# Column tiles of 64 or 32 for the plain products, and transposes in 64-row halves, in a four-layer transformer on one core

## The chip, the cores and the metric

The kernel runs on one core of a Trainium2 chip. A core has TensorE (PE; its weight loads are shown as PEld), VectorE (DVE), ScalarE (ACT), GpSimd (POOL) and SyncE (SP), which run side by side and wait for one another through semaphores. The metric is the device time of one execution in microseconds; the median of several runs is compared.

## The reference, cut to what matters

The input is `x`, 16 sequences of 256 tokens of 128 features, in float32. Four layers follow; each is an attention and a feed-forward part, both on the layer-normed `x` and both added to `x`.

```python
x = x + L0_attn(ln(x))   # 16 heads of 64, l2-normed q and k, ALiBi, causal, 2 null keys per head
x = x + L0_ffn(ln(x))    # gelu(x @ w1 + b1) @ w2 + b2, 512 wide
x = x + L1_attn(ln(x))   # 16 heads of 8 from a latent of 64, one shared k and v, causal
x = x + L1_ffn(ln(x))    # silu(w1 x) * (w2 x), two gelu layers of 512x512, w3
x = x + L2_attn(ln(x))   # 16 heads of 64, no mask, biases
x = x + L2_ffn(ln(x))    # each token through the best of 8 experts (relu, 512 wide)
x = x + L3_attn(ln(x))   # 16 heads of 8, causal, window of 128
x = x + L3_ffn(ln(x))    # token shift, sigmoid(r) * (relu(k)^2 @ W_v)
```

Layers 0 and 2 are called wide here (heads of 64), layers 1 and 3 narrow (heads of 8). All products are in float32.

## The kernel before, in words

Everything stays on the chip: the 4096 tokens lie in eight tiles `xg[g]` of two sequences each (a sequence is called a batch, `b`). Each batch of a layer goes through a preparation (`prep0` to `prep3`: layer norm, transpose of the normed tile by `turned`, projections to queries, keys and values), through units of heads (`wide_unit`, four per batch; `narrow_unit`, three per batch) and through an output step (`wide_out`, `narrow_out`; `out0` adds the null part of layer 0). After every second batch comes the feed-forward part of its tile (`feed0`, `feed1`, the gate and the experts in `Experts`, `mix`).

A unit has three kinds of work on TensorE: scores (queries against keys, contraction over 64 rows, or over 32 in the narrow layers), transposes of the probabilities, and products of transposed probabilities and values. Between them stand the softmax steps on DVE, ACT and POOL.

None of this is issued where it is written. Each piece is a `step` of the class `Plan`: an engine, a rank `p`, an estimated duration, the values that it reads and writes, and a function that emits its instructions. `Plan.run` (L132) builds one order for all engines from these: it follows the estimated times, gives out the buffers ("homes"), and takes the step that can start soonest, the lower rank first. PSUM is the home "t", eight banks of 512 columns. A step with the engine "AD" (the copies out of PSUM, `evac`, L392) may go to ACT or DVE, whichever the estimates favour.

A step of PE carries a mode, which names the tile of the 128x128 array that its matmuls use:

- "T": the whole array, 128 rows by 128 columns. All plain products (projections, feed-forward, experts, output) and the transposes of whole blocks are of this mode.
- "S": tiles of 64 rows. Wide scores and the half transposes of `turned_halves` (L367), which turn the upper and the lower 64 rows of a block into two different banks.
- "S4": tiles of 32 rows. Narrow scores.
- "O": tiles of 64 columns. Wide products of probabilities and values.
- "O4": tiles of 32 columns. Narrow products of probabilities and values.

Some matmuls have another shape than their step's mode says: the null part of layer 0, `nv_out` with 32 rows and its transposes to 32 partitions, lies inside "T" steps.

The planner counts `SWITCH` (130 ns) for a change of mode on PE, lets PE stay in its mode for a step up to `STAY` ranks later, and takes no step that is over `WINDOW` (12) ranks ahead of the first unfinished step of PE that is not of mode "T". `TURN` limits how far a step may take a buffer ahead of a lower-ranked step that is short of it.

All plain products go through one helper, and whole blocks are turned by one loop:

```python
def mm(o, lhsT, rhs, start=True, stop=True, **kw):
    nc.tensor.matmul(o, lhsT, rhs, start=start, stop=stop, **kw)
...
def turn(e):
    for i in range(nt):
        nc.tensor.transpose(t.t[:, i * P:(i + 1) * P], xn.t[:, i * D:(i + 1) * D], ident)
```

In the profile, L365 is the helper `mm`, L372 is `turned_halves`, L429 is the transpose in `turned`, L618 and L641 are those of `narrow_out`, L388 and L390 are the copies on ACT and DVE, L479 divides probabilities on POOL, L566 is the first softmax step of a narrow unit.

Of the kernel before, what the change touches and what calls it, by code (L numbers as in the profile page):

```python
# [67 lines left out]
class Plan:  # L68
# [11 lines left out]
    WINDOW, STAY, TURN, SWITCH = 12.0, 4.0, 3.0, 130  # L80
# [51 lines left out]
    def run(self):  # L132
        free = dict.fromkeys(self.SEEN, 0.0)
        ready = {e: [] for e in free}
        by_rank = sorted((s for s in self.steps if s.eng[0] == "PE" and s.mode != "T"), key=lambda s: (s.p, s.no))
        at, mode, left, window = 0, None, len(self.steps), self.WINDOW

# [25 lines left out]
        while left:  # L163
# [11 lines left out]
            for e, steps in ready.items():  # L175
# [12 lines left out]
                if e == "PE":  # L188
                    low = min(c[1] for c in could if c[0] <= soon + 40)
                    could = [(max(t, free[e] + self.SWITCH) if s.mode != mode else t, p, n, s) for t, p, n, s in could  # L190
                             if s.mode != mode or p <= low + self.STAY]
                    soon = min(could)[0]
# [18 lines left out]
            if e == "PE":  # L211
                mode = s.mode
# [19 lines left out]
def preln_d4_kernel(ctx: ExitStack, tc: tile.TileContext, x_in, vecs, rows, nullk, nullv,  # L232
# [127 lines left out]
    plan.home("small", many(sp, "small", 5, [256]))  # L360
    plan.home("pn", many(sp, "pn", 3, [2, 16, 2]))


    def mm(o, lhsT, rhs, start=True, stop=True, **kw):
        nc.tensor.matmul(o, lhsT, rhs, start=start, stop=stop, **kw)  # L365
# [57 lines left out]
    def turned(p, xn, nt, gamma=None):  # L423

        t, xnT = get("t"), get("xnT")

        def turn(e):
            for i in range(nt):
                nc.tensor.transpose(t.t[:, i * P:(i + 1) * P], xn.t[:, i * D:(i + 1) * D], ident)  # L429

        step("PE", p, 109 * nt, turn, r=[xn], w=[t], mode="T")
        n = nt * P
        if gamma is None:
            evac(p, xnT, t, lambda: (xnT.t[:, 0:n], t.t[:, 0:n]), n)
        else:
            step("ACT", p - 8, n * 0.83 + 145, lambda e: nc.scalar.activation(xnT.t[:, 0:n], t.t[:, 0:n], AF.Copy, scale=gamma),
                 r=[t], w=[xnT])
        return xnT
# [80 lines left out]
    def wide_out(p, b, st, w_out, more=None, reads=()):  # L519
        y = get("t")  # L520
        for qc in range(2):
# [8 lines left out]
            step("PE", p + 0.5 * qc, 1800 + (420 if more else 0), part, r=st["OT"] + list(reads), w=[y], mode="T")  # L530
# [81 lines left out]
    def narrow_out(p, b, st, w_proj):  # L612
# [3 lines left out]
        def turn(e):  # L616
            for i in range(4):
                nc.tensor.transpose(t.t[:, i * P:(i + 1) * P], oT.t[:, i * P:(i + 1) * P], ident)  # L618
# [18 lines left out]
        t2, yT = get("t"), get("small")  # L637

        def turn2(e):
            for qc in range(2):  # L640
                nc.tensor.transpose(t2.t[:, qc * P:(qc + 1) * P], o_sb.t[:, qc * P:(qc + 1) * P], ident)  # L641

        step("PE", p + 1, 218, turn2, r=[o_sb], w=[t2], mode="T")
        evac(p + 1, yT, t2, lambda: (yT.t[:, 0:256], t2.t[:, 0:256]), 256)
# [6 lines left out]
        step("PE", p + 2, 450, project, r=[yT], w=[y], mode="T")  # L651
# [44 lines left out]
    nv_out = cp.tile([32, D], F32, tag="nv_out", name="nv_out")  # L696
# [7 lines left out]
    def null2(e):  # L704
# [6 lines left out]
    step("PE", -13, 20, lambda e: nc.tensor.transpose(nk_ps.t[:, 0:16], nsq.rearrange("p j d -> p (j d)"), ident[0:16, 0:16]),  # L711
         r=["nss"], w=[nk_ps], mode="T")
# [9 lines left out]
    step("PE", 2, 2000, null3, w=[nv_ps], mode="T")  # L722
    step("DVE", 2, 200, lambda e: nc.vector.tensor_copy(nv_out, nv_ps.t[0:32, 0:D]), r=[nv_ps], w=["nv_out"])
# [3 lines left out]
    def prep0(b):  # L727
# [15 lines left out]
        def project(n, c):  # L743
# [6 lines left out]
                 r=[xnT], w=[ps], mode="T")  # L750
# [35 lines left out]
        def values(k):  # L786
# [3 lines left out]
                 r=[xnT], w=[ps], mode="T")  # L790
# [28 lines left out]
    def out0(b, st):  # L819
        p = first[0, b] + 12 + 13  # L820
        t, pnT = get("t"), get("small")

        def turn(e):
            for qc in range(2):
                nc.tensor.transpose(t.t[0:32, qc * P:(qc + 1) * P], st["pn"].t[:, qc].rearrange("p h n -> p (h n)"), ident)

        step("PE", p - 1, 218, turn, r=[st["pn"]], w=[t], mode="T")
        evac(p - 1, pnT, t, lambda: (pnT.t[0:32, 0:256], t.t[0:32, 0:256]), 256)
        wide_out(p, b, st, wout, lambda y, qc: mm(y[:, qc * P:(qc + 1) * P], pnT.t[0:32, qc * P:(qc + 1) * P], nv_out, False, True),
                 reads=[pnT, plan.key("nv_out")])  # L830
# [5 lines left out]
    def feed0(g):  # L836
# [9 lines left out]
        for c in range(4):  # L846
            ps = get("t")
            step("PE", lo + 6 + 2 * c, 862, lambda e, c=c, ps=ps: mm(ps.t, wA[:, o1 + c * P:o1 + (c + 1) * P], xnT.t),
                 r=[xnT, "wA"], w=[ps], mode="T")
# [8 lines left out]
        for i in range(4):  # L858
# [4 lines left out]
            step("PE", lo + 18 + i, 896, down, r=h + ["wA"], w=[y], mode="T")  # L863
# [3 lines left out]
    for b in range(B):  # L867
        st = prep0(b)

        def nulls_kept(p, u, pair, pr, st=st):  # L870

            def f(e):
                for qc, (a, z) in enumerate(parts0):
                    nc.gpsimd.tensor_copy(st["pn"].t[:, qc, 4 * u + 2 * pair:4 * u + 2 * pair + 2, :], pr.t[:, :, a:a + 2])
# [27 lines left out]
    def prep1(b):  # L902
# [6 lines left out]
        step("PE", lo + 5, 431, lambda e: mm(ps.t[:, 0:256], wl[:, at1["down"]:at1["down"] + P], xnT.t[:, 0:256]), r=[xnT], w=[ps], mode="T")  # L909
# [7 lines left out]
        step("PE", lo + 6, 862, both, r=[lat], w=[ps2], mode="T")  # L917
# [8 lines left out]
        step("PE", lo + 7, 450, values, r=[lat], w=[ps3], mode="T")  # L926
# [18 lines left out]
    def feed1(g):  # L945
# [8 lines left out]
        for c in range(4):  # L954
# [11 lines left out]
            step("PE", p, 1724, up, r=[xnT, "w1", f"h2.{g - 1}"], w=[pa, pb], mode="T")  # L966
# [4 lines left out]
        def layer(name, sname, src, p):  # L971
            dst = [get("r") for _ in range(4)]
            for o in range(4):
                ps = get("t")
                for half in range(2):
# [4 lines left out]
                    step("PE", p + 2 * o + half, 1724, hidden, r=src, m=[ps], w=[f"{name}.{g}"], mode="T")  # L980
# [531 lines left out]
```

## Time and profile before

| what | us |
|---|---|
| median of 3 runs (2195.37 to 2201.18) | 2196.09 |
| the profiled execution | 2192.15 |
| its span, first to last instruction | 2190.5 |
| PE busy, 26001 matmul records | 2097.8 |
| ACT busy | 1695.0 |
| DVE busy | 1633.5 |
| POOL busy | 1049.6 |

The times of single stages come from one profiled execution. A matmul in float32 leaves two records, one for each of two passes, and a transpose one. Records of matmuls overlap, since they are pipelined: the distance from one start to the next tells how long the array was taken, and the duration does not. By the scores, layer 0 runs from about 47 to 630 us of the span, layer 1 to 1133, layer 2 to 1816 (its second half of experts to about 1985, beside the beginning of layer 3), and layer 3 to the end.

### The profile page before, as it was taken

The page shows a single profiled execution, that of the slowest core. Times are in us where ns is not written, and L with a number is a line of the kernel's source. Part 1 is how long each engine was busy: PE and PEld are TensorE (multiplying, and loading weights), DVE is VectorE, ACT ScalarE, POOL GpSimd, SP SyncE. Part 2 cuts the span into 40 slices and gives each one's busy share as a digit, 9 for nine tenths or more (in the row PEclk, how much of TensorE's full clock was granted, in tenths as well). Part 3 has the DMA queues.
Part 4 walks back from the last instruction along what each step waited for, and adds up shares of the span by engine and source line. Part 5 has one row for each costly group of instructions (what it writes and reads, how often), then busy time and mean ns, then how long its engine had stood idle before and what let it go on. Part 6 is the DMA issues. An engine that isn't in the chain of part 4 may idle for free. (4 is left out here: it accounts for less than half of the span.)

```text
span 2190.5 us, 68042 instructions
## 1 busy us (share of the span) xinstructions
PE 2097.8 (96%) x26001; PEld 1519.2 (69%) x26001; DVE 1633.5 (75%) x6363; ACT 1695.0 (77%) x4798; POOL 1049.6 (48%) x2019
## 2 busy tenths in 40 slices
PE   5999999999999999999999999999999999998996
PEld 3667777776776555555566677888888786786664
DVE  5898898889888666556655456767665788887996
ACT  4898889889889877678667667777766677777995
POOL 5997798788851111111113335554443855226331
PEclk9999999999999999999999999999999999999998
DMA  8000000000000000000000000000332000451000
GB/s 188 32 2 2 2 2 2 2 2 2 30 13 3 2 2 2 2 2 2 2 1 2 1 2 7 7 6 5 119 112 84 26 5 19 138 163 30 12 13 12
DMA packets 58488, 57.92 MB, mean 26 GB/s; under 512 B 27809, under 2 KB 48817, under 8 KB 58161
## 3 DMA queue, kind: packets, MB, share of 16 engines
q1 hardware_dynamic: 55360, 48.54, 7.9%
q8 instruction: 205, 3.36, 0.7%
q0 software_dynamic: 2048, 4.20, 0.6%
q14 instruction: 123, 1.00, 0.2%
q10 hardware_dynamic: 752, 0.83, 0.1%
HBM read 43.32 MB, written 10.22 MB: 24 GB/s over the span
## 5 line engine op out<-in xcount | busy, mean ns | idle before, releaser
L447 POOL TENSOR_TENSOR x<-x,row_sb 128x256 f32<-128x256 f32 x48 | 35.0, 730 | 43.8 <-DVE xn0x L416 18.5
L409 POOL TENSOR_SCALAR ln_rs2x<-ln_mv2x 128x2 f32<-128x2 f32 x21 | 4.0, 191 | 72.6 <-DVE ln_mv2x L405 71.9
L409 POOL TENSOR_SCALAR ln_rs3x<-ln_mv3x 128x2 f32<-128x2 f32 x23 | 4.4, 191 | 68.1 <-DVE ln_mv3x L405 63.9
L409 POOL TENSOR_SCALAR ln_rs1x<-ln_mv1x 128x2 f32<-128x2 f32 x23 | 5.2, 226 | 64.9 <-DVE ln_mv1x L405 63.9
L409 POOL TENSOR_SCALAR ln_rs4x<-ln_mv4x 128x2 f32<-128x2 f32 x23 | 4.4, 191 | 65.3 <-DVE ln_mv4x L405 60.9
L409 POOL TENSOR_SCALAR ln_rs0x<-ln_mv0x 128x2 f32<-128x2 f32 x22 | 4.2, 191 | 64.8 <-DVE ln_mv0x L405 63.4
L1001 POOL TENSOR_TENSOR x<-x,sq1x 128x512 f32<-128x512 f32 x4 | 5.1, 1266 | 62.4 <-DVE sq1x L999 62.4
L479 POOL TENSOR_SCALAR probs4x<-probs4x,sums2x 128x256 f32<-128x256 f32 (+2 forms) x44 | 23.0, 536 | 25.0 <-DVE sums2x L474 18.1
L376 POOL TENSOR_TENSOR ss0x<-ss0x,mhalf 128x16 f32<-128x16 f32 x11 | 32.0, 2909 | 5.7 <-DVE ss0x L756 4.3
L376 POOL TENSOR_TENSOR ss1x<-ss1x,mhalf 128x16 f32<-128x16 f32 x11 | 32.3, 2938 | 2.8 <-DVE ss1x L756 2.7
L376 POOL TENSOR_TENSOR ss2x<-ss2x,mhalf 128x16 f32<-128x16 f32 x11 | 31.9, 2902 | 3.6 <-DVE ss2x L756 3.1
L376 POOL TENSOR_TENSOR ss3x<-ss3x,mhalf 128x16 f32<-128x16 f32 x11 | 32.2, 2930 | 0.1
L479 POOL TENSOR_SCALAR probs4x<-probs4x,sums4x 128x256 f32<-128x256 f32 (+2 forms) x44 | 20.3, 475 | 24.7 <-DVE sums4x L474 24.3
L479 POOL TENSOR_SCALAR probs0x<-probs0x,sums6x 128x256 f32<-128x256 f32 (+2 forms) x44 | 19.2, 453 | 25.8 <-DVE sums6x L474 18.7
L479 POOL TENSOR_SCALAR probs4x<-probs4x,sums6x 128x256 f32<-128x256 f32 (+2 forms) x40 | 17.6, 454 | 27.2 <-DVE sums6x L474 19.9
L479 POOL TENSOR_SCALAR probs2x<-probs2x,sums6x 128x256 f32<-128x256 f32 (+2 forms) x44 | 19.4, 455 | 23.2 <-DVE sums6x L474 16.0
L376 POOL TENSOR_TENSOR ss5x<-ss5x,mhalf 128x16 f32<-128x16 f32 x10 | 29.8, 2979 | 1.3 <-DVE ss5x L756 1.2
L479 POOL TENSOR_SCALAR probs0x<-probs0x,sums2x 128x256 f32<-128x256 f32 (+2 forms) x40 | 18.6, 478 | 24.4 <-DVE sums2x L474 24.3
L376 POOL TENSOR_TENSOR ss4x<-ss4x,mhalf 128x16 f32<-128x16 f32 x10 | 29.0, 2900 | 2.4 <-DVE ss4x L756 2.0
L479 POOL TENSOR_SCALAR probs2x<-probs2x,sums4x 128x256 f32<-128x256 f32 (+2 forms) x40 | 19.2, 491 | 22.5 <-DVE sums4x L474 22.1
L479 POOL TENSOR_SCALAR probs2x<-probs2x,sums2x 128x256 f32<-128x256 f32 (+2 forms) x44 | 21.0, 490 | 15.7 <-DVE sums2x L474 15.5
L479 POOL TENSOR_SCALAR probs2x<-probs2x,sums0x 128x256 f32<-128x256 f32 (+2 forms) x44 | 19.6, 460 | 17.1 <-DVE sums0x L474 14.8
(4452 smaller groups left out, 10747.5 us busy)
## 6 DMA issues: line engine op xcount, KB each, us to landing
w0x<-in_wex_dram SPq DMA_DIRECT2D x16, 578.0 KB, 3.9
w1x<-in_wex_dram SPq DMA_DIRECT2D x15, 578.0 KB, 4.1
w2x<-in_wex_dram SPq DMA_DIRECT2D x15, 578.0 KB, 4.0
w_wA<-in_wa_dram SPq DMA_DIRECT2D x8, 512.0 KB, 5.7
ex_rows<-zero SPq DMA_DIRECT2D x2, 1472.0 KB, 22.4
x<-in_x_dram SPq DMA_DIRECT2D x8, 256.0 KB, 7.8
w_wB<-in_wb_dram SPq DMA_DIRECT2D x4, 512.0 KB, 6.6
xs0x<-ex_rows SPq DMA_DIRECT2D x16, 64.0 KB, 3.7
```

What stands on the lines that cost most here:

```text
L376: nc.gpsimd.tensor_tensor(t, t, mhalf[:t.shape[0]].broadcast_to([t.shape[0], n]), ALU.pow)
L409: nc.gpsimd.tensor_scalar(ln.t[2], ln.t[1][:, :, 1], LN_EPS, 1.0, ALU.add, ALU.mult)
L447: step("POOL", p, 670, lambda e: nc.gpsimd.tensor_tensor(x_of(b), x_of(b), row_over(name, 2), ALU.add), r=reads, m=[X[b]])
L479: nc.gpsimd.tensor_scalar(pr.t[:, j, a:z], pr.t[:, j, a:z], sums.t[:, i:i + 1], 1.0, ALU.mult, ALU.mult)
L1001: step("POOL", lo + 30, 1300, lambda e: nc.gpsimd.tensor_tensor(x, x, ys.t.rearrange("p (c d) -> p c d", d=D), ALU.add), r=[ys, "w1"], m=xx)
```

## The change

The mode "T" of the plain products becomes a mode "P", which has no tile of its own. When such a step is taken, it uses the column tiles that PE is already in (64 columns in "O", 32 in "O4"); if PE is in another mode, it uses that of the next unfinished products of probabilities and values. `mm` then issues each product as two or four matmuls, one for each column tile, on the same moving data. `flip` turns a block in column tiles by a product with the identity; the transposed tokens of the experts use it.

```diff
+    COLUMNS = {"O": 64, "O4": 32}
+    WINDOW, STAY, TURN, SWITCH = 20.0, 4.0, 4.0, 180
-    WINDOW, STAY, TURN, SWITCH = 12.0, 4.0, 3.0, 130
...
-        by_rank = sorted((s for s in self.steps if s.eng[0] == "PE" and s.mode != "T"), key=lambda s: (s.p, s.no))
+        by_rank = sorted((s for s in self.steps if s.eng[0] == "PE" and s.mode != "P"), key=lambda s: (s.p, s.no))
...
+        def tiling(s):
+
+            if s.mode != "P":
+                return s.mode
+            return mode if mode in self.COLUMNS else next((x.mode for x in by_rank[at:] if x.end is None and x.mode in self.COLUMNS), "O")
...
+    def parts(n):
+
+        w = plan.COLUMNS.get(plan.mode, P)
+        return [slice(a, min(n, a + w)) for a in range(0, n, w)]
 
     def mm(o, lhsT, rhs, start=True, stop=True, **kw):
-        nc.tensor.matmul(o, lhsT, rhs, start=start, stop=stop, **kw)
+        for c in parts(o.shape[0]):
+            nc.tensor.matmul(o[c], lhsT[:, c], rhs, start=start, stop=stop, **kw)
+
+    def flip(o, block):
+
+
+        i = ident[0:block.shape[0], 0:block.shape[0]]
+        if plan.mode in plan.COLUMNS:
+            mm(o, block, i)
+        else:
+            nc.tensor.transpose(o, block, i)
```

The transposes of whole blocks become half transposes of mode "S", each into two banks with two copies out: those of `turned` (all layer norms), of `mix`, of `out0` and the second ones of `narrow_out`. The first ones of `narrow_out` (L618) keep the mode "T" and the whole array.

```diff
+    def in_halves(p, src, n, out_of):
+
+        t = [get("t"), get("t")]
+
+        def turn(e):
+            for i in range(n):
+                turned_halves(t, 64 * i, src[1](i))
+
+        step("PE", p, 62 * n, turn, r=[src[0]], w=t, mode="S")
+        return [(t[z], lambda z=z: t[z].t[:, 0:64 * n].rearrange("p (i q) -> p i q", q=64),
+                 lambda z=z: out_of().rearrange("p (i z q) -> p i z q", z=2, q=64)[:, :, z]) for z in range(2)]
...
     def turned(p, xn, nt, gamma=None):
...
+        xnT = get("xnT")
+        for t, src, dst in in_halves(p, (xn, lambda i: xn.t[:, i * D:(i + 1) * D]), nt, lambda: xnT.t[:, 0:nt * P]):
+            if gamma is None:
+                evac(p, xnT, t, lambda src=src, dst=dst: (dst(), src()), nt * 64)
```

The null part is padded from 32 to 128 rows with zeros: `pn` has 128 columns for each half of the queries, `nv_out` 128 rows. To make room, "pn" has two buffers for three and "small" four for five.

```diff
-    plan.home("small", many(sp, "small", 5, [256]))
-    plan.home("pn", many(sp, "pn", 3, [2, 16, 2]))
+    plan.home("small", many(sp, "small", 4, [256]))
+    pn = many(sp, "pn", 2, [2, P])
+    for t in pn:
+        nc.gpsimd.memset(t, 0.0)
+    plan.home("pn", pn)
...
-    nv_out = cp.tile([32, D], F32, tag="nv_out", name="nv_out")
+    nv_out = cp.tile([P, D], F32, tag="nv_out", name="nv_out")
+    nc.gpsimd.memset(nv_out, 0.0)
```

All other edits put "P" for "T" in the steps of the plain products.

## The prediction

> **What bounds the kernel now.** I read the page's busy times first, then the table by stretches (cut where the layers begin), then PE's waits, and last PE's timeline in three stretches.
>
> ```profile
> PE 2097.8 (96%) x26001; PEld 1519.2 (69%) x26001; DVE 1633.5 (75%) x6363; ACT 1695.0 (77%) x4798; POOL 1049.6 (48%) x2019
> ```
>
> TensorE is the busiest engine by 400 us, but its ends are modelled, so 96% does not say how much of it is streaming. The table by stretches says where the others are close behind (columns: busy us and instructions of each engine, granted clock, DMA share, GB/s):
>
> ```profile
> 47.00:630.00 583.00, 574.98 (x6702) 419.46 (x6700) 517.79 (x1939) 518.27 (x1596) 487.03 (x930) 0.99 0.04 10
> 630.00:1133.00 503.00, 495.50 (x6107) 297.99 (x6107) 333.82 (x1567) 377.66 (x857) 67.68 (x92) 1.00 0.01 3
> 1133.00:1816.00 683.00, 668.79 (x7047) 537.82 (x7036) 440.60 (x1199) 482.94 (x1528) 335.87 (x691) 0.99 0.10 30
> 1816.00:1985.00 169.00, 160.89 (x2619) 128.45 (x2619) 143.81 (x715) 127.90 (x352) 49.91 (x91) 0.96 0.35 106
> 1985.00:2190.00 205.00, 173.92 (x3443) 123.29 (x3432) 174.95 (x893) 169.17 (x437) 84.06 (x139) 0.94 0.06 16
> ```
>
> Layers 1 and 2 (rows two and three) are TensorE's alone: DVE and ACT are at 65 to 75%. In layer 0 (row one) DVE and ACT are at 89% each and POOL at 84%, so a faster TensorE soon meets them. Layer 3 (the last two rows) has TensorE at 95 and 85%: it is already bound by latency and DVE in part.
>
> ```profile
> PE t0x L365 <- DMA w_wA<-in_wa_dram: 20.2, 1, 20.2
> PE t0x L372 <- POOL probs2x L479: 4.2, 1, 4.2
> PE t1x L365 <- DVE pT0x L390: 2.2, 2, 1.3
> ```
>
> After the 20 us for the first weights, no wait of PE is over 4.2 us. What TensorE loses is elsewhere, in the timeline (start, duration, then partitions*columns of the array tile that is used):
>
> ```profile
> 251.39 0.39 PE L365 MATMUL t3x<-w_wA,r0x 128*128 128x128 f32 x2
> 251.61 0.39 PE L365 MATMUL t3x<-w_wA,r5x 128*128 128x128 f32 x2
> 251.93 0.44 PE L365 MATMUL t5x<-pT2x,V2x 128*64 128x128 f32 x4
> 252.20 0.39 PE L365 MATMUL t5x<-pT3x,V2x 128*64 128x128 f32 x4
> 252.41 0.28 PE L365 MATMUL t5x<-pT2x,V3x 128*64 128x64 f32 x4
> ...
> 253.20 0.29 PE L365 MATMUL t5x<-pT1x,V3x 128*64 128x64 f32 x4
> 253.42 0.27 PE L372 MATMUL t4x<-ident,probs0x 64*128 64x64 f32 x1
> ...
> 253.53 0.22 PE L372 MATMUL t4x<-ident,probs0x 64*128 64x64 f32 x1
> ...
> 253.59 0.22 PE L372 MATMUL t4x<-ident,probs0x 64*128 64x64 f32 x1
> ```
>
> Starts are the thing to read. Inside one tile shape they are even: a full-array product of 128 columns every 0.22 us, two 64-column tiles together (x4: two products in two passes) every 0.21, a pair of half transposes every 0.06. Where the shape changes there is a hole: the last full product would free the array at 251.61+0.22 = 251.83, the next starts at 251.93, and its follower comes 0.27 later instead of 0.21: 0.10+0.06. From 64-column tiles to half transposes: 253.20+0.12 = 253.32, start 253.42, follower 0.11 later instead of 0.06: 0.15. **A change of shape costs about 0.16 us**, with nothing to wait for.
>
> ```profile
> 701.45 1.02 PE L365 MATMUL t3x<-xnT0x,w_wB 128*128 128x512 f32 x2
> 702.40 0.32 PE L365 MATMUL t5x<-pT2x,q2x 128*32 128x64 f32 x8
> 702.53 0.29 PE L365 MATMUL t5x<-pT3x,q2x 128*32 128x64 f32 x8
> ```
>
> Four 32-column tiles (x8) of 64 moving columns start every 0.11 us. A full-array product of 64 columns would take half of the 0.22 above, 0.11 also. So column tiles lose nothing: two or four run side by side.
>
> **The change, part by part.** *Shape changes.* Counted in the built order of TensorE's matmuls by tile shape, neighbours of different shape go from 1006 to 685. By layer: 322 to 146, 233 to 186, 202 to 134, 249 to 219. At 0.16 each the 321 are 51 us.
>
> *The null part* in layer 0 is 32 products over 32 rows, each between two changes:
>
> ```profile
> 163.50 0.61 PE L365 MATMUL t3x<-w_wA,OT3x 128*128 128x128 f32 x4
> 164.03 0.48 PE L365 MATMUL t3x<-nv_out,small2x 32*128 32x128 f32 x2
> 164.45 0.71 PE L365 MATMUL t3x<-w_wA,OT0x 128*128 128x128 f32 x4
> 165.00 0.61 PE L365 MATMUL t3x<-w_wA,OT1x 128*128 128x128 f32 x4
> ```
>
> From 163.50+0.45 = 163.95 to 164.45, and 0.10 more for the follower (0.55 for 0.45): 0.60 us. Padded to 128 rows it is one more full product, 0.22. Saved 0.38 x 32 = 12 us, which contains 64 of layer 0's 176 removed changes; the other 112 are 18 us.
>
> *Transposes in halves.* A whole 128x128 transpose starts every 0.11 us in the trace (four in 0.49 from 704.91, 0.05 of it start-up), a pair of halves every 0.06. Per layer: layer 0 has 16 batches x 2, 8 feeds x 4 and 16 x 2 of the null part: 96 x 0.05 = 5 us; layer 1 has 96 too (batches, feeds, the second transposes of `narrow_out`), 5 us; layer 2 (batches, gates) 64, 3 us; layer 3 (batches, mixes, `narrow_out`) 96, 5 us. Against it the 46 expert blocks' transposes become products with the identity, 0.22 for 0.11: 5 us lost in layer 2.
>
> *Plain products in column tiles.* 17104 matmul instructions become 21702. Those of 128 columns cost 0.218 a pair of tiles (eight groups of that kind in a row at 1300.73 to 1302.31 start every 0.22) against 0.223: I take 0 to 0.006 gain on some 1400, 0 to 8 us, and book 4, in layers 0 and 2 above all. Those of 512 columns in column tiles are in no row. Bounds: as even as the 64 and 128-column ones (nothing), or with no overlap at all (rival three). I take nothing: the row with four tiles is the nearest, as it issues eight matmuls in 0.11 us, a far denser stream than eight in 0.86.
> The Trainium skill, "TensorEngine Tiling (Array Packing)", section Instruction Overhead, speaks against this part: each matmul has some 60 cycles of overhead, and a tiling factor should not be taken from a dimension that is already small. At the 2.4 GHz of its page "TensorE: Matmul & The Clock Gate" that would be an estimated 25 ns for each of the 4598 new instructions, 115 us, and the forecast would turn into a loss of some 66. The trace disagrees: eight matmuls in 0.11 us are 14 ns each, and the stream is not longer than without tiles.
>
> *Copies out of PSUM.* Each transpose in halves takes two banks and two copies for one: 144 more copies (109 on DVE, 35 on ACT, counted in the built order). By rows: a 128x128 copy on ACT means 273 ns, a 128x256 one 386, so a split adds up to 0.16, 23 us over two engines and the whole span, some 5 us to each in layer 0. Besides, 84 copies of probabilities and outputs move from ACT (0.59) to DVE (0.68): mostly in layers 1 and 2, where DVE has a quarter to a third free. On the path this is nothing there. ACT's table loads stay 49. The two clears of pn and the one of nv_out are POOL's before the weights land, under the 20 us wait.
>
> *The planner's numbers* (WINDOW 20, TURN 4, SWITCH 180) are in the counts above; "small" loses a buffer and "pn" one. No queue of SP is touched.
>
> **Sum for TensorE:** layer 0: 12+18+5+2 = 37; layer 1: 47 x 0.16+5 = 13; layer 2: 68 x 0.16+3-5+2 = 11; layer 3: 30 x 0.16+5 = 10. Total 71. On the path: layers 1 and 2 almost whole, less 1 each for the waits that exist: 12 and 10. Layer 0: TensorE would drop to about 546 us while DVE and ACT need 518 and some 5 more, 96%; three engines do not mesh so closely through eight banks, and in the built order TensorE's next use of a bank stands nearer to the copy that empties it than before. I take 60%, 22 us; bounds 0 and 37. Layer 3: half, 5 us. Sum 49. The profiled execution took 2192.15 (span 2190.5), which gives 2143; the median of the runs shown, 2196.09, lies 4 above it, so **2147**.
>
> **Rivals.** (1) *Other engines take layer 0.* For it: 89% of DVE and ACT. Then layer 0 gives nothing: 12+10+5 = 27, time 2169. Chance 0.22.
> (2) *Slower: banks.* A half transpose wants two free banks at once, and longer bursts of one shape ask for them faster. If the bursts of half-array work in layers 0 and 3 (about 72+71 after the change) each wait for one ACT copy of 512 columns more, 0.60 us, that is 86 us against 71: 2196+15 = 2211. It decides from about 118 such waits on. Against it: PE's waits are short now. Chance 0.12. With waits that just eat the gain the time is within 0.3%: 0.07.
> (3) *It does not do what it says:* column tiles of 512 moving columns run one after the other. About 616 such products of 0.86 would take at least twice that, +530 us: near 2720. Against it: the two timelines above. Chance 0.03.
>
> **How the numbers follow.** Forecast 0.56. Faster: 0.56+0.22 = 0.78; same 0.07; slower 0.15. What a measurement can tell from no change is about 0.3%, 6.6 us. Range: all 71 on the path is 2125, and 20 of TensorE's 73 idle us (2190.5-2097.8 less the first 20) gone with them 2105; the upper end takes in rival one and no gain at all, 2195. Outside are the slower cases and a few in a hundred below.
>
> **What would show it.** In the profile after: no hole between plain products and 64- or 32-column products; 512-column tiles (x4 or x8) starting every 0.86 us; layer 0's stretch shorter by about 22 us with DVE and ACT above 91%; layers 1 and 2 by 12 and 10. Wrong it is if tiles of 512 start more than 0.9 apart, or if PE's waits on copies out of PSUM add up to tens of us.

## The result, and the profile after

The changed kernel takes **2191.64 us** (median of 14 runs, 2188.01 to 2193.68) against 2197.65 for the kernel before (14 runs beside them, 2194.52 to 2201.18). The ratio is 0.9968, with a 95% interval of 0.9960 to 0.9976: faster by 6 us, a third of a per cent, where 49 were forecast. The profiled execution of it took 2188.83 us, with a span of 2187.1.

The first line of the page (busy us, share of the span, instructions of each engine):

```profile
PE 2063.7 (94%) x34892; PEld 1411.2 (65%) x34892; DVE 1678.9 (77%) x6472; ACT 1668.8 (76%) x4833; POOL 1061.8 (49%) x2022
```

TensorE is busy 34 us less than before, but the span is only 3.4 us shorter. Its idle time rose from 93 to 123 us. The table by stretches, cut at the same events as before (columns as there), says where:

```profile
48.00:634.00 586.00, 562.00 (x7996) 405.32 (x7996) 522.37 (x1966) 519.50 (x1622) 499.83 (x927) 0.98 0.03 10
634.00:1131.00 497.00, 486.36 (x9262) 254.98 (x9258) 353.39 (x1600) 363.18 (x855) 70.29 (x98) 1.00 0.01 4
1131.00:1805.00 674.00, 653.30 (x9032) 498.91 (x9028) 463.43 (x1230) 470.10 (x1516) 338.00 (x694) 0.98 0.10 31
1805.00:1985.00 180.00, 167.27 (x4512) 126.68 (x4508) 145.12 (x749) 134.60 (x376) 61.03 (x107) 0.96 0.34 104
1985.00:2187.00 202.00, 168.20 (x3936) 113.20 (x3936) 172.88 (x875) 162.04 (x432) 68.68 (x118) 0.90 0.05 13
```

Layer 0 (row one) is not shorter at all: TensorE's busy time fell by 13 us and its idle time rose from 8 to 24. Layers 1 and 2 are shorter, by 7 and 8.5 us. Layer 3 is longer by 8.

What was built works as it should. TensorE's timeline in layer 0 (start, duration, the tile of the array), from half transposes over two projections to products of probabilities and values:

```profile
284.60 0.22 PE L410 MATMUL t3x<-ident,probs2x 64*128 64x64 f32 x1
284.62 0.22 PE L410 MATMUL t0x<-ident,probs2x 64*128 64x64 f32 x1
284.77 1.08 PE L382 MATMUL t5x<-w_wA,xnT1x 128*64 128x512 f32 x4
285.68 1.03 PE L382 MATMUL t4x<-w_wA,xnT1x 128*64 128x512 f32 x4
286.54 0.39 PE L382 MATMUL t6x<-pT2x,V0x 128*64 128x128 f32 x4
286.76 0.39 PE L382 MATMUL t6x<-pT3x,V0x 128*64 128x128 f32 x4
```

The second projection takes 286.54-285.68 = 0.86 us and the next product follows at once, with no hole between 512 and 128 columns. Between the half transposes and the first projection the hole is still there. In layer 1 the same holds for four tiles, x8 and x16:

```profile
700.00 1.04 PE L382 MATMUL t7x<-xnT1x,w_wB 128*32 128x512 f32 x8
700.86 1.04 PE L382 MATMUL t4x<-xnT1x,w_wB 128*32 128x512 f32 x8
701.72 1.04 PE L382 MATMUL t5x<-xnT1x,w_wB 128*32 128x512 f32 x8
702.57 0.62 PE L382 MATMUL t1x<-wl,small0x 128*32 128x128 f32 x16
703.01 0.29 PE L382 MATMUL t3x<-pT2x,q0x 128*32 128x64 f32 x8
```

To see where the time went I cut TensorE's matmuls of each trace into bursts of one tile shape and took the distance from the first start of a burst to the first start of the next. Of it, "stream" is what its matmuls take at the even distances of the rows above; the excess up to 0.20 us is booked as the change of shape; what is over that is waiting. Stream that started while the granted clock was 0.5 is taken out of the waiting as "slow clock". The numbers of changes are counted in the records, of which some are missing, and so lie a little under the built order's. In layer 3 what follows the last burst is counted as waiting. A wait that ends at a change of shape gives its first 0.20 us to the change, and the split moves by a few us with the even distances that are taken for the rarer shapes. Change from before to after, in us:

| layer | length | stream | changes (number) | waiting | slow clock |
|---|---|---|---|---|---|
| 0 | +3.2 | +2.0 | -32.1 (315 to 138) | +25.7 | +7.7 |
| 1 | -6.7 | -4.7 | -10.7 (233 to 186) | +7.0 | +1.7 |
| 2 | -8.5 | -3.7 | -12.5 (202 to 134) | +4.6 | +3.1 |
| 3 | +7.7 | -2.3 | -6.2 (248 to 218) | +11.4 | +4.8 |
| all | -4.3 | -8.7 | -61.5 | +48.7 | +17.3 |

So TensorE's own work became some 70 us shorter, close to the 71 of the forecast, and 66 came back: 49 as waits and 17 as slow clock.

One such wait, in full. After's timeline of all engines (in brackets the idle time before, and who ended it):

```profile
289.15 0.71 POOL L414 TENSOR_TENSOR ln_rs4x<-ln_rs4x,mhalf 128x2 f32<-128x2 f32 x1
289.90 0.60 DVE L454 TENSOR_SCALAR xn1x<-x,ln_mv4x,ln_rs4x 128x128 f32<-128x128 f32 x2 [1.95 <-POOL ln_rs4x L414]
...
291.25 0.29 DVE L835 CUSTOM_DVE_ANT_0 probs0x<-t1x,dist 128x130 f32<-128x130 f32 x1
...
291.64 0.41 ACT L843 ACTIVATE probs0x<-probs0x,nm10x 128x130 f32<-128x130 f32 x1 [1.66 <-DVE nm10x L835]
...
291.95 0.27 PE L410 MATMUL t1x<-ident,xn1x 64*128 64x64 f32 x1 [1.02 <-DVE nm10x L835]
```

DVE stands 1.95 us at a layer norm whose inverse root POOL delivers late. Behind it in DVE's queue, after the statistics of another layer norm, stands the reading of the scores in bank t1. Only when that is done (nm10) may ACT take the exponentials and TensorE turn the next normed tile into t1. Summed over layer 0 (the waits view; us in total, times, longest), before:

```profile
DVE sums7x L474 <- ACT probs1x L814: 4.1, 3, 2.5
DVE pT5x L390 <- PE t0x L372: 2.3, 1, 2.3
...
DVE ss3x L759 <- POOL ss3x L376: 1.7, 2, 0.9
DVE xn0x L416 <- POOL ln_rs3x L376: 1.6, 1, 1.6
```

and after:

```profile
DVE ss4x L788 <- POOL ss4x L414: 3.5, 4, 1.6
DVE ss0x L788 <- POOL ss0x L414: 3.4, 3, 1.6
DVE ss2x L788 <- POOL ss2x L414: 3.3, 4, 1.6
...
DVE xn1x L454 <- POOL ln_rs2x L414: 2.3, 2, 1.9
```

Before, the longest are not for POOL (first two lines), and those for POOL come below them; after, those for POOL lead. All of DVE's waits for POOL's inverse roots (`ss` for the norms of queries and keys, `ln_rs` for the layer norms) make 12.5 us in layer 0 before and 31 after. DVE does not idle longer for it: all its waits there make 59 us both times, since those for TensorE fell from 37 to 20.5. It now waits for POOL where it waited for TensorE.

### The profile page after: what moved, and what is told of

It reads as the page before. It is cut to its first block, busy times and chain, and to the rows that moved or that the text cites. A ratio compares the mean times of both kernels' runs of the same rounds, so it can differ in the third digit from the quotient of the medians.

```text
span 2187.1 us, 86099 instructions
## 1 busy us (share of the span) xinstructions
PE 2063.7 (94%) x34892; PEld 1411.2 (65%) x34892; DVE 1678.9 (77%) x6472; ACT 1668.8 (76%) x4833; POOL 1061.8 (49%) x2022
## 5 line engine op out<-in xcount | busy, mean ns | idle before, releaser
L511 POOL TENSOR_SCALAR probs2x<-probs2x,sums0x 128x256 f32<-128x256 f32 (+2 forms) x44 | 20.3, 477 | 30.5 <-DVE sums0x L506 15.3
L511 POOL TENSOR_SCALAR probs0x<-probs0x,sums4x 128x256 f32<-128x256 f32 (+2 forms) x44 | 20.6, 481 | 27.7 <-PE t6x L382 14.6
L1025 POOL TENSOR_TENSOR x<-x,sq0x 128x512 f32<-128x512 f32 x4 | 5.1, 1278 | 56.5 <-DVE sq0x L1023 56.5
L511 POOL TENSOR_SCALAR probs4x<-probs4x,sums2x 128x256 f32<-128x256 f32 (+2 forms) x44 | 21.7, 512 | 20.9 <-DVE sums2x L506 10.3
L511 POOL TENSOR_SCALAR probs4x<-probs4x,sums0x 128x256 f32<-128x256 f32 (+2 forms) x40 | 18.4, 475 | 15.7 <-DVE sums0x L506 7.9
```

The costliest lines, as they stand in the source:

```text
L511: nc.gpsimd.tensor_scalar(pr.t[:, j, a:z], pr.t[:, j, a:z], sums.t[:, i:i + 1], 1.0, ALU.mult, ALU.mult)
L1025: step("POOL", lo + 30, 1300, lambda e: nc.gpsimd.tensor_tensor(x, x, ys.t.rearrange("p (c d) -> p c d", d=D), ALU.add), r=[ys, "w1"], m=xx)
```

## The experiments

The theories. **Order**: the change saves TensorE what was forecast, but the planner's new numbers (WINDOW, TURN, SWITCH) build an order that loses it again. **Neighbours**: in layer 0 POOL, DVE and ACT set the pace, so a change of shape removed there returns as a wait whatever the order. **Tiles or halves**: one of the two edits costs something that I had not priced. Ratios are to the kernel before on the same chip, with 95% intervals. The runs lie on several chips, on which the kernel before takes 2192.15 to 2198.96 us, so kernels from different chips are compared by their ratios (the changed kernel: 0.9968). Lengths of layers are from the one profiled execution of each kernel.

**The changed kernel with the old numbers.**

```diff
-    WINDOW, STAY, TURN, SWITCH = 20.0, 4.0, 4.0, 180
+    WINDOW, STAY, TURN, SWITCH = 12.0, 4.0, 3.0, 130
```

> The changed kernel with the planner's old numbers (WINDOW 12, TURN 3, SWITCH 130); changes of tile shape 743 for 685. Others-pace theory (in layer 0 DVE, ACT and POOL together set the pace, so TensorE's saved time becomes waiting): layer 0 stays at 580 to 590 us, total 2185 to 2200. Order theory (the longer window and the dearer change build bursts that then wait): layer 0 falls to about 560, total 2150 to 2170. Bank theory (two banks and two copies for each half transpose eat the gain): same as now, 2185 to 2200.

2180.12 us, ratio 0.9937 (0.9920 to 0.9954). The old numbers leave more changes of shape (743 in the built order against 685), and yet the kernel is some 7 us faster than with the new ones (0.9937 against 0.9968). Layer 0 takes 582.2 us, in the range of the theory of the neighbours and far from the 560 of the theory of the order.

**The kernel before with the new numbers.**

```diff
-    WINDOW, STAY, TURN, SWITCH = 12.0, 4.0, 3.0, 130
+    WINDOW, STAY, TURN, SWITCH = 20.0, 4.0, 4.0, 180
```

> The kernel before with the planner's new numbers alone (WINDOW 20, TURN 4, SWITCH 180); changes of shape 973 for 1006, 33 fewer, 5 us by the row. Others-pace theory: layer 0 unchanged at about 583, total 2188 to 2200. Order theory: slower, 2215 or more, as the waits come with the numbers. Bank theory: 2188 to 2200.

2178.2 us, ratio 0.9924 (0.9908 to 0.9941). The numbers alone, without tiles or halves, are worth 15.6 us, with 973 changes for 1006. This beats both kernels, and no theory had it in its range. So "the new numbers are bad" is wrong as a rule: they help the old code and hurt the new. Read the other way, tiles and halves together gain 14 us with the old numbers (1 to 0.9937) and lose 10 with the new ones (0.9924 to 0.9968).

**Tiles without half transposes** (new numbers; `turned`, `mix` and `narrow_out` turn whole blocks again):

```diff
-        for t, src, dst in in_halves(p, (xn, lambda i: xn.t[:, i * D:(i + 1) * D]), nt, lambda: xnT.t[:, 0:nt * P]):
...
+                nc.tensor.transpose(t.t[:, i * P:(i + 1) * P], xn.t[:, i * D:(i + 1) * D], ident)
+
+        step("PE", p, 109 * nt, turn, r=[xn], w=[t], mode="T")
```

> The changed kernel with whole transposes of whole blocks again (one bank, one copy, full array) in the layer norms, the mixes and the outputs of the narrow layers; plain products stay in column tiles; 794 changes of shape. Others-pace theory: layer 0 at 580 to 590, total 2190 to 2205. Order theory: the same within 10 of the changed kernel's 2192. Bank theory: faster, layer 0 below 570 and the total below 2175, though there are 109 more changes of shape (17 us).

2185.77 us, ratio 0.9969 (0.9957 to 0.9981); layer 0 takes 582.5 us.

**Half transposes without tiles** (new numbers; a plain product uses the whole array and counts as a shape of its own):

```diff
-            if s.mode != "P":
-                return s.mode
-            return mode if mode in self.COLUMNS else next((x.mode for x in by_rank[at:] if x.end is None and x.mode in self.COLUMNS), "O")
+            return "T" if s.mode == "P" else s.mode
```

> The changed kernel with plain products on the full array again; half transposes, padding and the new planner numbers stay; 847 changes of shape. Others-pace theory: layer 0 at 580 to 590, the rest between before and after, total 2190 to 2200. Order theory: 2195 to 2215. Bank theory: slower than before, 2205 to 2220, as the banks are paid and only half of the changes are saved.

2183.42 us, ratio 0.9951 (0.9934 to 0.9968); layer 0 takes 580.5 us. Either half of the change on top of the new numbers lies above the numbers alone (0.9924; by 8 and 5 us on the same chip, the second with intervals that still touch), and both together are no better. Neither of the two edits is the one culprit.

**Less work for TensorE** (half of the output products of the wide layers left out, in the kernel before and in the changed one):

```diff
-                for c in range(8):
+                for c in range(4):
...
-                       c == 0, c == 7 and more is None)
+                       c == 0, c == 3 and more is None)
...
-            step("PE", p + 0.5 * qc, 1800 + (420 if more else 0), part, r=st["OT"] + list(reads), w=[y], mode="T")
+            step("PE", p + 0.5 * qc, 900 + (420 if more else 0), part, r=st["OT"] + list(reads), w=[y], mode="T")
```

> The kernel before, with half of the output products of the wide layers left out (4 of 8 chunks): 16 batches x 2 x 4 x 0.223 = 28.5 us less on TensorE in layer 0 and as much in layer 2; the other engines' work is the same. Others-pace theory: layer 0 falls by less than 8 us from 583, layer 2 by 20 to 28 from 682. If TensorE paces layer 0: both fall by 20 to 28.

> The same omission in the changed kernel. Others-pace theory: layer 0 stays at 580 to 587, layer 2 falls by 10 to 25 from 674. If TensorE paces: 20 to 28 in both.

One execution each, beside 2198.67 for the kernel before: 2150.31 and 2145.36. The edit takes some 28.5 us of stream (128 products at 0.223) from each wide layer. Layer 0 became shorter by 17.2 and 17.7 us, layer 2 by 28.6 and 26.3. So in layer 2 TensorE's work counts in full, and in layer 0 at 60%, before and after alike. Layer 0 is not closed to a faster TensorE; but its changes of shape did not count like its stream. The planner ordered both kernels anew, so order has a part in these numbers too: layer 3, which the edit leaves alone, moved by 6.2 and 3.5 us.

**Less work for DVE and ACT in layer 0** (the squares of queries and keys on ACT and their sums on DVE replaced by a small fill on DVE):

```diff
-            step("ACT", p, 520, lambda e: nc.scalar.activation(sq.t, raw.t, AF.Square), r=[raw], w=[sq])
-            step("DVE", p, 592, lambda e: nc.vector.tensor_reduce(ss[n].t[:, c * 8:(c + 1) * 8], sq.t.rearrange("p (h d) -> p h d", d=64),
-                                                                  AX.X, ALU.add), r=[sq], w=[ss[n]])
+            step("DVE", p, 60, lambda e: nc.vector.memset(ss[n].t[:, c * 8:(c + 1) * 8], 1.0), r=[raw], w=[ss[n]])
```

> The kernel before, without the squares (ACT, 128 x 0.52 = 67 us) and their sums (DVE, 128 x 0.59 = 76 us) of layer 0's norms; a small clear of the sums on DVE stands in their place. Others-pace theory with DVE and ACT at the bottom: layer 0 falls to where TensorE stops it, some 555 to 565 (stream 484, 314 changes at 0.16, 20 to 30 of rest). If TensorE paces layer 0: 575 to 583, no fall over 10.

> The same relief of DVE and ACT in the changed kernel. Others-pace theory with DVE and ACT: layer 0 falls by 40 or more, to 520 to 545, so here the saved changes of shape count and the changed kernel's layer 0 is 20 us or more below that of the kernel before under the same relief. If POOL paces: both stay at 575 or more. Order theory: no more than 15 lower.

2185.55 and 2177.39, beside 2198.67. Layer 0: 576.1 and 576.8 us. The changed kernel is still not the shorter one there, with about 9 points of DVE's and ACT's load gone. Both stay at 575 or more, as was expected if POOL paces the layer.

**Less work for POOL in layer 0** (the inverse roots of `ss`, 2.9 us each, left out):

```diff
-                step("POOL", p - 6, 2892, lambda e: rsqrt(ss[n].t, 16), m=[ss[n]])
```

> The kernel before, without POOL's inverse roots of the sums of squares in layer 0 (64 x 2.9 = 187 us of POOL, and the wait that DVE's scaling has for them). If POOL and the waits for it set layer 0's pace: layer 0 falls from 583 to 555 to 568, where TensorE with its 310 changes of shape stops it. If not: 575 to 583, as without the squares on ACT and DVE (576).

> The same relief of POOL in the changed kernel. POOL theory: layer 0 falls further than in the kernel before, to 525 to 550, and lies 15 to 30 us below it. If not: 570 to 587, within 8 us of the kernel before under the same relief.

2182.59 and 2162.87, beside 2193.49. Layer 0: 573.3 and 565.4 us. Now the changed kernel is ahead in layer 0, by 7.9. Both fell less far than the POOL theory said (555 to 568 and 525 to 550) and further than was expected without it (575 to 583 and 570 to 587): POOL has a part, and not the whole.

**Both reliefs together.**

> The kernel before with both reliefs, no squares and sums on ACT and DVE and no inverse roots on POOL in layer 0. TensorE must be the limit then: stream 484, 300 changes at 0.16 = 48, and 15 to 30 of rest: layer 0 at 547 to 562.

> The changed kernel with both reliefs. If a change of shape is worth 0.16 us where TensorE is the limit: stream 487, 146 changes 23, 15 to 30 of rest: layer 0 at 525 to 540, 20 to 30 below the kernel before under the same reliefs. If the price of a change was wrong (it hides in other waits anyway), the two lie within 10.

2167.58 and 2134.32, beside 2193.49. Layer 0: 568.0 and 551.4 us. By the table of stretches, layer 0 of the relieved kernel before:

```profile
38.00:606.00 568.00, 568.00 (x6716) 417.01 (x6714) 472.75 (x1995) 454.66 (x1438) 330.41 (x870) 1.00 0.05 12
```

and of the relieved changed kernel:

```profile
40.00:591.00 551.00, 546.77 (x8034) 396.94 (x8030) 465.81 (x1994) 465.40 (x1487) 323.17 (x866) 1.00 0.05 13
```

TensorE has no gap at all in the first, 4 us in the second, and full clock in both. Both layers are longer than expected (547 to 562 and 525 to 540), and 16.6 us lie between them for the 20 to 30 expected. In the relieved changed kernel DVE still waits 36 us for POOL's inverse roots of the layer norms (9.5 in the other one). The longest:

```profile
DVE xn1x L454 <- POOL ln_rs4x L414: 7.2, 3, 2.8
```

The series for layer 0, where the last two columns hold what changed from the kernel before to the changed one under the same relief ("waiting" with its slow clock):

| left out | length, before and after | waiting, before and after | difference of waiting | of length |
|---|---|---|---|---|
| nothing | 583.3, 586.5 | 25.2, 58.6 | +33.4 | +3.2 |
| DVE's and ACT's part | 576.1, 576.8 | 20.9, 45.6 | +24.7 | +0.7 |
| POOL's part | 573.3, 565.4 | 15.3, 34.3 | +19.0 | -7.9 |
| both | 568.0, 551.4 | 8.8, 19.5 | +10.7 | -16.6 |

The more of the neighbours' work goes, the more of the saved 30 us arrives; with both gone it is 55% of it, about the share that the forecast had assumed for the kernel as it is. POOL's part alone opens more than DVE's and ACT's. The orders of these kernels differ somewhat too, so a single row is a weak witness; the sequence is the evidence.

**The changed order, with full-array products.** The planner runs as in the changed kernel, and each product of 128 output rows is issued on the whole array:

```diff
         w = plan.COLUMNS.get(plan.mode, P)
+        if n == P:
+            w = P
```

> The changed kernel in its own order, step for step, but every plain product of 128 outputs uses the whole array, so that the changes of shape rise from 685 to 920 (layers: 146 to 214, 186 to 245, 134 to 213, 219 to 248). Hidden theory (a change that is saved comes back as a wait for the other engines): within 12 of the changed kernel, 2180 to 2204, and the waits of over 0.2 us fall by most of what the changes take. Price theory (each change is worth its 0.19 us at a given order, and the gain was lost by the new order): 235 x 0.19 = 45 slower, 2225 to 2240.

2208.23 us, ratio 1.0081 (1.0064 to 1.0097) against 0.9968: some 25 us slower than the changed kernel, between the two theories. This is the cleanest comparison, since every engine has the same order. Its layers 0 to 2 in the table of stretches:

```profile
46.00:634.00 588.00, 571.07 (x6825) 424.06 (x6824) 523.46 (x1968) 521.46 (x1622) 498.08 (x928) 0.99 0.04 10
634.00:1144.00 510.00, 499.65 (x6202) 296.42 (x6200) 354.13 (x1599) 364.37 (x856) 69.68 (x97) 1.00 0.01 3
1144.00:1832.00 688.00, 670.75 (x7112) 536.88 (x7108) 466.27 (x1230) 470.76 (x1515) 336.23 (x694) 0.99 0.10 30
```

Layers 1 and 2 are 12.6 and 14.5 us longer for 59 and 79 more changes: 0.21 and 0.18 us each, the full price. Layer 0 has 68 more changes that cost 13.6 us, and 13.7 us less waiting: 1.6 longer in all, which is about its stream's difference (505.0 to 503.3). In this order a change of shape in layer 0 is free, as far as one execution of each can tell. Layer 3 goes the other way: with 29 more changes it is 7.5 us shorter (374.5 to 382.0), by less waiting. The kernel's waits of DVE in layer 0 are those of the changed kernel, almost to the tenth:

```profile
DVE ss0x L790 <- POOL ss0x L416: 3.4, 3, 1.6
DVE ss4x L790 <- POOL ss4x L416: 3.3, 4, 1.6
DVE ss2x L790 <- POOL ss2x L416: 3.2, 4, 1.6
```

All of DVE's waits for POOL's inverse roots in layer 0 make 28 us here and 31 in the changed kernel. So DVE's standing behind POOL comes with the order that was built for the changed kernel, and not from a faster TensorE.

**Single numbers taken back in the changed kernel**: WINDOW to 12, and in another kernel SWITCH to 130.

```diff
-    WINDOW, STAY, TURN, SWITCH = 20.0, 4.0, 4.0, 180
+    WINDOW, STAY, TURN, SWITCH = 12.0, 4.0, 4.0, 180
```

> The changed kernel with WINDOW 12 alone taken back (TURN 4, SWITCH 180 stay); 697 changes of shape. If the window sets the extra waits: 2178 to 2184, as with all three numbers taken back (2180). If the price of a change in the planner does: 2188 to 2196, as the changed kernel.

```diff
-    WINDOW, STAY, TURN, SWITCH = 20.0, 4.0, 4.0, 180
+    WINDOW, STAY, TURN, SWITCH = 20.0, 4.0, 4.0, 130
```

> The changed kernel with SWITCH 130 alone taken back (WINDOW 20, TURN 4 stay); 728 changes of shape. If the planner's price of a change builds the bursts that wait: 2178 to 2184. If the window does: 2188 to 2196.

2192.44 us, ratio 1.0002 (0.9992 to 1.0012), and 2204.83, ratio 1.0056 (1.0039 to 1.0073). By the ratios, taking all three back gains 7 us on the changed kernel, taking back WINDOW alone loses 7, and SWITCH alone 19, outside both of its ranges. The numbers have no effects of their own that could be added up: each set makes another order, and the kernels with the full computation lie between 0.9906 and 1.0081 of the kernel before, 38 us apart.

**Old numbers, and whole transposes in layer 3 alone**, since layer 3 had become longer:

```diff
-        xnT = turned(lo + 3, xn, 2)
+        xnT = turned_whole(lo + 3, xn, 2)
...
-        narrow_out(first[3, b] + 8 + 13, b, st, w3("out"))
+        narrow_out(first[3, b] + 8 + 13, b, st, w3("out"), whole=True)
```

> The changed kernel with the planner's three old numbers, and in layer 3 alone whole transposes again (one bank, one copy). Put together from what the runs so far gave: layer 0 582, layer 1 498, layer 2 670, layer 3 372 to 378 for 385, total 2166 to 2174. If layer 3's longer waits have nothing to do with the half transposes there: 2176 to 2184.

2179.07 us, ratio 0.9906 (0.9890 to 0.9923), which also beats both kernels and can't be told from the kernel before with the new numbers. Layer 3 stayed at 384.6 us (385.3 without the edit): it is as long without half transposes of its own. Layers 0 to 2 have the same order in both of these kernels, and their lengths differ by 2.9, 1.6 and 2.3 us; smaller differences of a layer's length say nothing.

All orders with the full computation, sorted by the changes of shape in layer 0 (us, one profiled execution each; "waiting" with slow clock):

| kernel | changes | their cost | waiting | sum | length of layer 0 |
|---|---|---|---|---|---|
| before | 315 | 56.7 | 25.2 | 81.9 | 583.3 |
| before, new numbers | 303 | 54.5 | 25.5 | 80.0 | 579.6 |
| after's order, full array | 206 | 38.2 | 44.9 | 83.1 | 588.1 |
| halves only | 192 | 35.5 | 40.0 | 75.5 | 580.5 |
| after, old numbers | 174 | 30.7 | 47.3 | 78.0 | 582.2 |
| mixed | 174 | 30.7 | 44.4 | 75.1 | 579.3 |
| tiles only | 173 | 30.5 | 48.0 | 78.5 | 582.5 |
| after, SWITCH 130 | 156 | 27.9 | 67.2 | 95.1 | 598.5 |
| after, WINDOW 12 | 144 | 25.8 | 60.8 | 86.6 | 590.7 |
| after | 138 | 24.6 | 58.6 | 83.2 | 586.5 |

The cost of the changes halves down the table, and the sum does not fall with it: it lies between 75 and 95.

## Why the prediction was wrong in size

**What held.** *The price of a change of shape*: 0.16 forecast; the median excess per burst was 0.195 in the kernel before, and at a constant order a change was worth 0.21 and 0.18 us in layers 1 and 2. *Tiles of 512 columns side by side*: 0.86 us for x4 and x8 (rival three is out). *TensorE's sum*: 37, 13, 11 and 10 by layer were forecast; changes and stream together gave 30.1, 15.4, 16.2 and 8.5, in all 70 for 71, with layer 0 some 7 short. There the stream grew by 2.0 us, and it now holds the 32 padded null products too, 7 us at 0.22 each. *No price per instruction*: TensorE has 8891 more matmul records and 8.7 us less stream. The forecast's reason for it was misread: the eight in 0.11 us are records, two for each product, so four products at 28 ns and not eight at 14. A row of the gate in the profile after shows shorter ones (columns as before):

```profile
1825.79 0.44 PE L382 MATMUL t4x<-gw_sb,xnT0x 128*32 128x8 f32 x31
1826.06 0.40 PE L382 MATMUL t1x<-xnT1x,w_wC 128*32 128x256 f32 x1
```

These 31 records in four column tiles take 0.27 us, 17 ns for each product of two records. The Trainium skill ("TensorEngine Tiling (Array Packing)", section Instruction Overhead) gives some 60 cycles for each matmul; the 115 us that the forecast had estimated from it for the added ones are not seen here.

*Copies*: DVE's and ACT's extra load in layer 0 was 4.6 and 1.2 us, where 5 each were booked.

**The step that failed** is the path in layer 0: "I take 60%, 22 us". The layer became 3 us longer. In its place the runs show waiting: at one and the same order, 68 more changes of 13.6 us in layer 0 were met by 13.7 us less waiting. The 60% itself was a fair guess for products left out (17 of 28.5 us), but the holes at the changes counted for nothing. Why the two differ is not shown; my reading is that the neighbours catch up in the 57 us of holes of the kernel before. I had named DVE and ACT at 89% and counted only their load. What I overlooked is that each engine takes its work in the order built: DVE late by 2 us behind one inverse root of POOL holds back the scores of another head, and their bank. POOL at 84% I read off and then left out of the argument. The relief series bears it out: POOL's part gone brings more than DVE's and ACT's. Even with both gone, 45% of the saving stays away; how much of that is the order and how much POOL's layer norms is open.

**The second step** that failed is "layers 1 and 2 almost whole", 12 and 10 us: they gave 6.7 and 8.5. At a constant order they do give the full price (12.6 for 59 changes, 14.5 for 79). Against the kernel before, the order is another one, and 8.7 and 7.7 us of waiting and slow clock came with it. I priced the planner's numbers at nothing because their changes of shape were in the counts; their waits were not. Alone they gained 15.6 us in the kernel before and cost 7 in the changed one.

**The third** is "layer 3: half, 5 us": it became 8 us longer, by 16 us of waiting and slow clock. Its length is 372 to 375 us in four of the ten orders above (before, before with new numbers, tiles only, after's order with the full array) and 378 to 385 in the other six. The planner's numbers do not sort these groups. The half transposes do with two exceptions: after's order with the full array has them and is short (374.5), and the mixed kernel has none in layer 3 and is long (384.6). But the layer also moves with no edit of its own. In the three relieved changed kernels, which leave out work of layer 0 alone (and so carry other data), DVE and ACT have the same order in layer 3 as in the changed kernel (buffer numbers aside); the layer takes 385.9, 378.1 and 372.3 us there, for 382.0. So in single executions 8 us can't be put down to any edit, and the cause in layer 3 stays open.

**The signs I had named.** No hole between plain products and the 64 or 32-column ones, and 512-column tiles every 0.86: seen. Layer 0 shorter with DVE and ACT above 91%: not seen, they stand at 89%, as before. PE's waits on copies out of PSUM in tens of us, named as what would prove it wrong: that came in part. TensorE idles 16 us more in layer 0; its waits for copies out of PSUM there rose from 3.8 to 10.3 us, and all its waits for DVE from 4.6 to 19.0. The three longest in after's layer 0 (columns as before) all stand before a half transpose (L410). Two are at banks that DVE was late to read, to copy them or for the scores; the third is for `r6x` itself, which DVE scales by one of POOL's inverse roots:

```profile
PE t2x L410 <- DVE Q1x L428: 1.7, 1, 1.7
PE t1x L410 <- DVE nm12x L835: 1.7, 1, 1.7
PE t2x L410 <- DVE r6x L796: 1.4, 1, 1.4
```

**The rivals.** Rival one (other engines take layer 0; 2169) was right for its layer, and would still have been 23 us off, as it left layers 1 to 3 at the gains forecast. Rival two had the place right (a half transpose waiting for a bank) and the engine wrong: TensorE's waits in layer 0 after are 2.7 us for ACT and 19.0 for DVE, in part behind POOL; with 66 us eaten for 71 it came within some 5 us of turning the sign. The case of "waits that just eat the gain" lies nearest. The time is 3 us inside the upper end of the range.

## What to carry to other kernels

Ask what a closed hole on the busiest engine is worth in each stage. Here a change of shape was worth its full 0.18 to 0.21 us in two layers with DVE and ACT at 65 to 75%, and nothing in the layer with them and POOL at 84 to 89%, where it came back as waits. Price work taken from the busiest engine and holes taken from it as separate terms: here the first counted at 60% in that layer and the second not at all, though the two were measured on different orders. When an edit goes through a planner, compare at a constant order first, and then ask what other orders cost and how far a stage moves with no edit of its own: here a change of three planner numbers alone gained more (15.6 us) than 321 removed changes of shape with the order they came in (6).

## What the hardware showed that I had not expected

TensorE's granted clock falls to one half for short windows in the middle of layer 0, with TensorE 96% busy over the layer. There are five of 3.4 us in after's trace, at 294.7, 369.8, 448.3, 523.4 and 601.9; the kernel before has none between 75 and 1723 us. The table of stretches around the first (columns as before; the last but two is the clock):

```profile
284.70:288.10 3.40, 3.40 (x49) 2.12 (x46) 3.19 (x8) 2.60 (x7) 3.40 (x8) 1.00 0.02 5
288.10:291.50 3.40, 2.83 (x60) 2.54 (x60) 1.53 (x9) 1.85 (x3) 3.14 (x10) 1.00 0.00 0
291.50:294.70 3.20, 2.17 (x29) 1.76 (x31) 3.20 (x19) 3.06 (x10) 3.03 (x11) 1.00 0.00 0
294.70:298.10 3.40, 3.40 (x35) 3.17 (x33) 3.23 (x20) 2.38 (x10) 1.98 (x5) 0.51 0.01 2
```

TensorE was idle for 1.6 of the 6.6 us before the window (the wait shown above lies there), and then fully busy at half speed. Its timeline across the end of the window:

```profile
296.89 0.64 PE L382 MATMUL t0x<-pT5x,V0x 128*64 128x128 f32 x4
297.32 0.43 PE L382 MATMUL t0x<-pT4x,V1x 128*64 128x64 f32 x4
...
298.17 0.39 PE L382 MATMUL t0x<-pT1x,V0x 128*64 128x128 f32 x4
298.39 0.28 PE L382 MATMUL t0x<-pT0x,V1x 128*64 128x64 f32 x4
```

A pair of tiles with 128 columns takes 0.43 us at first, and 0.22 after it. Where such a window follows a wait, the wait is paid twice: once as idle time, once as up to 1.7 us of slow stream behind it. The last 3.4 us before the five windows have TensorE 46 to 64% busy; but 3.4 us at 59% from 137.7 and again from 212.8 were followed by full clock, so the busy share alone does not decide it, and what does stays open. Over the span the windows at half clock grew from 62.6 to 102.4 us. The Trainium skill ("TensorE: Matmul & The Clock Gate", section Part 1: The HAM clock gate) ties the lower clock to a whole idle window of about 3.4 us; here no single idle stretch before it was over 1.3 us (290.7 to 291.95), and the measurement decides.
